# Message products of a graph network on two 64-column halves of TensorE, in place of 128 columns at once

## The chip, the core and the metric

The kernel runs on one NeuronCore of a Trainium2 chip. The core's engines work side by side, each through its own list of instructions: TensorE (PE) multiplies matrices on an array of 128 x 128 cells, with results in PSUM; VectorE (DVE) and ScalarE (ACT) work element by element; GpSimd (POOL) does a little of the same; SyncE (SP) starts DMA transfers. Semaphores order them. A matmul is two instructions, the load of its stationary operand (LDWEIGHTS, shown as PEld) and the multiplication that streams the moving operand through (MATMUL, shown as PE). The metric is the device time of the whole program in microseconds.

## What is computed

There are 16 graphs of 1024 nodes with 128 features, and each has its own 1024 x 1024 adjacency matrix. A first small network and a norm make `x` from the inputs. Then four layers follow, which have the same form and, in the third and fourth, wider inputs (features of earlier layers are put beside):

```python
IN_DIMS = [128, 128, 256, 384]
def _layer(nodes, adj, ws, bs, wd, bd, wn, bn, wu, bu):
    src = nodes @ ws + bs
    src_agg = jnp.einsum('bjv,bij->biv', src, _l2norm(adj, 2))
    dst = nodes @ wd + bd
    dst_agg = jnp.einsum('bjv,bji->biv', dst, _l2norm(adj, 1))
    self_rep = nodes @ wn + bn
    upd = jnp.concatenate([src_agg, self_rep, dst_agg], axis=2)
    return jnp.tanh(upd @ wu + bu)
...
x = _layernorm(x + _L1_gnn_ref(x, adj, ...), axis=-1)
```

All of it is in float32. The kernel folds `wu` into `ws`, `wd` and `wn` once, so that a layer is: **messages** (nodes times folded weights plus bias, 256 values for each node: 128 for the destination's sum and 128 for the source's), then the **aggregation** (messages times adjacency, both directions, plus the nodes' own part), then tanh.

## The kernel before

Per graph, TensorE goes through: messages of the first layer, aggregation, messages of the second, aggregation, messages of the third, aggregation, the first small network of the *next* graph, messages of the fourth, aggregation. Constants: `P = 128`, `V = 64`, `HW = 512`, `NJ = 4`, `CHUNKS = [1, 1, 2, 3]` (128-wide parts of a layer's input).

A helper issues one product as two, each for 64 of its 128 stationary columns. The output's partitions choose the half of the array:

```python
def by_halves(out, x, y, start=True, stop=True):
    for s in (slice(V, P), slice(V)):
        nc.tensor.matmul(out[s], x[:, s], y, start=start, stop=stop)      # L183
```

It serves several small sums (`pm`, `pv`, `pc`, `rp`, 32 columns to stream) and the weights of the small network (`pw`, 512 columns).

The messages. The stationary operand is 128 nodes of the features `f`, the moving one the 256 columns of the folded weights `wm`. Each group `g` makes two blocks of 128 nodes in one PSUM bank, which DVE reads when it adds the bias:

```python
def messages(b, l, feats, wm, between={}, with_sums=True):
    nch = CHUNKS[l]
    t = [one.tile([P, NJ, 2, 2, V], F32, tag=f"t{j}", ...) for j in range(2)]
    for n, g in enumerate((2, 3, 0, 1)):
        pt = ps_t.tile([P, 2, 2 * P], F32, tag="pt", ...)                 # ps_t: 4 banks
        for q in range(2):
            i = 2 * g + q
            for k, (f, c) in enumerate(feats):
                nc.tensor.matmul(pt[:, q], f[:, i * P:(i + 1) * P], wm[:, 1 + c],
                                 start=(k == 0), stop=(k == nch - 1))     # L605
        j, o = divmod(2 * g, NJ)
        nc.vector.tensor_add(t[j][:, o:o + 2]..., pt, wm[:, 0]...)        # L608
        if n in between:
            between[n]()
    ...
    for part in (DST, SRC):                                               # S3, L620
        nc.vector.tensor_sub(S[3][:, :, part], X[0, 0][:, :, part], X[1, 0][:, :, part])
    nc.vector.tensor_add(S[1], X[1, 0], X[1, 1])
    nc.vector.tensor_sub(S[2], S[1], X[0, 0])
    nc.vector.tensor_sub(S[4], X[0, 1], S[2])
    return X, S
```

The groups 2 and 3 need the second half of the nodes' features, 0 and 1 the first half.

The aggregation (Strassen's scheme in Winograd's form, with 64 message columns as one block) issues its products in pairs, one for each 64-column half of the array, with 512 columns to stream:

```python
def aggregate(b, l, feats, msgs, a, at, T, Q, fT, etag, hooks={}, pieces=1):
    ...
    upper = [(Z1, True, own(1, 1)), (Z0, True, own(1, 0)), (A, True, prod("M1", DST) + ...), ...]
    lower = [(Z1, True, own(0, 1)), (Z0, True, own(0, 0)), ...]
    up, lo = flat_steps(upper, high), flat_steps(lower, low)      # high: partitions 64..127
    for i, pair in enumerate(zip(up, lo)):
        if i - 2 * n in events:
            events[i - 2 * n]()            # DVE and ACT read finished products
        if i in hooks:
            hooks[i]()                     # work for other stages and the next graph
        for o, x, y, start, stop in pair:
            nc.tensor.matmul(o, x, y, start=start, stop=stop)             # L774
    nc.vector.tensor_add(e0, e0, Z0)                                      # L776
    squash(l, 0, e0, fT)                   # tanh of the first half on ACT, L787
```

It begins with the nodes' own part (`own`, one to three pairs for each half of the nodes), which needs no messages. The second half of the features is squashed before the aggregation ends, the first half after it.

The first graph's first layer alone is done by `plain_layer`, with products of 128 stationary columns (L653). The engines' instructions stay in the order in which the program issues them (`manual_schedule`).

Of the kernel before, what the change touches and what calls it, by code (L numbers as in the profile page):

```python
# [14 lines left out]
P = 128  # L15
# [8 lines left out]
def adj_resnorm_kernel(ctx: ExitStack, tc: tile.TileContext, x, adj, w0, b0, layers, out):  # L24
# [33 lines left out]
    nc = tc.nc  # L58
# [62 lines left out]
    def message_tile(name):  # L121

        return one.tile([P, 4, 2 * P], F32, tag="wm", name=name)
# [48 lines left out]
    def message_weights(b, l):  # L172
        wm = message_tile(f"wm{l + 1}_{b}")
        nc.sync.dma_start(wm[:, :CHUNKS[l] + 1], wsave[l])
        return wm

    def small(name, shape=(K,)):
        return ps_s.tile([P, *shape], F32, tag="small", name=name)
# [5 lines that stand above are left out]
# [411 lines left out]
    def messages(b, l, feats, wm, between={}, with_sums=True):  # L595


        nch = CHUNKS[l]
        t = [one.tile([P, NJ, 2, 2, V], F32, tag=f"t{j}", name=f"t{l + 1}_{b}_{j}") for j in range(2)]
        for n, g in enumerate((2, 3, 0, 1)):  # L600
            pt = ps_t.tile([P, 2, 2 * P], F32, tag="pt", name=f"pt{l + 1}_{b}_{g}")
            for q in range(2):
                i = 2 * g + q
                for k, (f, c) in enumerate(feats):
                    nc.tensor.matmul(pt[:, q], f[:, i * P:(i + 1) * P], wm[:, 1 + c],  # L605
                                     start=(k == 0), stop=(k == nch - 1))
            j, o = divmod(2 * g, NJ)
            nc.vector.tensor_add(t[j][:, o:o + 2].rearrange("p k a v c -> p k (a v c)"), pt,  # L608
                                 wm[:, 0][:, None, :].to_broadcast([P, 2, 2 * P]))
            if n in between:  # L610
                between[n]()
        if not with_sums:
            return t


        S = {i: one.tile([P, NJ, 2, V], F32, tag=f"S{i}", name=f"S{i}_{l + 1}_{b}") for i in (2, 3, 4)}
        X = {(v, j): t[j][:, :, :, v] for v in range(2) for j in range(2)}
        S[1] = X[1, 0]
        for part in (DST, SRC):
# [5 lines that stand above are left out]
# [203 lines left out]
    wm = message_tile("wm1_0")  # L828
# [27 lines left out]
    pt = small("w0tr", [HW])  # L856
# [139 lines left out]
    for b in range(B):  # L996
# [8 lines left out]
        if b == 0:  # L1005
            def row_factors0():
# [3 lines left out]
                for q in (2, 3):  # L1010
                    scale_rows(rows[q], q, rinv)

            t = messages(b, 0, feats, wm, {0: lambda: to_x1(0), 2: row_factors0}, with_sums=False)
            cinv = {}

# [42 lines left out]
            wm = message_weights(b, 1)  # L1058
            a2 = load(n)
            xs2 = load_spread(n)  # L1060
        else:
            w = {}
            if nxt:
                w["a"] = load(n)
                st = begin_sums(n)
            t = messages(b, 0, feats, wm)
            wm = message_weights(b, 1)
            Q = combined(b, "Q")
# [22 lines left out]
        feats = [(f1, 0)]  # L1091
        f23 = feature(b, "f23T")
        t = messages(b, 1, feats, wm)
        wm = message_weights(b, 2)

# [106 lines left out]
        wm = message_weights(b, 3)  # L1202
# [92 lines left out]
        if nxt:  # L1295
            wm = message_weights(n, 0)
# [60 lines left out]
```

## Time and profile before

| | |
|---|---|
| median of 3 runs | 2456.7 us (2456.55 to 2457.03) |
| span of the profiled run | 2454.6 us |
| TensorE's mean granted clock | 1.000 |
| TensorE busy | 2433.6 us (99%), 11453 matmul rows |
| LDWEIGHTS | 1026.5 us (42%), 11453 rows |
| DVE busy | 1909.8 us (78%) |
| ACT busy | 956.8 us (39%) |
| DMA | 41.3% of 16 engines for the data queue, 90 GB/s on average |
| messages (L605) | 1792 matmul rows of 128x256, mean 379 to 386 ns; loads of 128 columns, 190 ns |
| aggregation (L774) | rows of 128x512 on 64 columns, mean 592 to 602 ns; loads of 64 columns, 137 ns |

In a line of a group, `128*64` is the stationary operand's rows and columns, `128x512` the shape of what streams, then the number of rows, the busy time and the mean duration of one, the idle time of the engine just before them and who ended it. A float32 product of the program stands in the trace as two rows. Durations of matmuls overlap, since the next one starts before the last has left the array; the distance of two starts tells what one costs in a sequence. A load can run under the streaming of the matmul before it.

### The profile page before, as it was taken

To read this page: it belongs to the slowest core of one execution; us is meant where nothing else is said; L and a number is where in the kernel's file an instruction comes from. 1 tells how busy PE (TensorE), PEld (TensorE's weight loads), DVE (VectorE), ACT (ScalarE), POOL (GpSimd) and SP (SyncE) were. 2 spreads that over 40 slices of the span, in tenths; PEclk is the share of its full clock that TensorE was granted. 3 is DMA by queue.
4 is the path that set the end of the run, shared out by engine and by line. 5 is a ranking of instruction groups with operands and counts; after the bars stand their busy time and mean duration, and the time that the engine had idled before them with its cause. 6 is when DMAs were issued, how large, how long until landed. Compare 5 with 4: busy or idle time off the path is not lost.

```text
span 2454.6 us, 30806 instructions
## 1 busy us (share of the span) xinstructions
PE 2433.6 (99%) x11453; PEld 1026.5 (42%) x11453; DVE 1909.8 (78%) x2495; ACT 956.8 (39%) x1794; POOL 287.2 (12%) x100
## 2 busy tenths in 40 slices
PE   8999999999999999999999999999999999999998
PEld 5443344433444344443434434334443344433444
DVE  5878878798786878868788687887878878697743
ACT  5415334263342624335144351533515334262321
POOL 4101111101111011111011110111100111101100
PEclk9999999999999999999999999999999999999999
DMA  9517254261633517235172352724427254261410
GB/s 207 105 46 150 52 116 89 63 132 44 138 75 74 113 44 160 62 82 104 44 155 59 83 104 59 144 54 102 90 64 140 49 123 90 61 126 44 95 24 9
DMA packets 365717, 219.69 MB, mean 90 GB/s; under 512 B 152768, under 2 KB 336832, under 8 KB 365568
## 3 DMA queue, kind: packets, MB, share of 16 engines
q1 hardware_dynamic: 364800, 215.36, 41.3%
q0 software_dynamic: 768, 2.36, 0.4%
q8 instruction: 91, 1.49, 0.3%
q14 instruction: 58, 0.48, 0.1%
HBM read 199.17 MB, written 18.46 MB: 89 GB/s over the span
## 4 chain that ended last, share of the span: by engine, by line
PE 84%; DVE 6%; DMA 5%; SPq 1%; ACT 1%; issue 1%; DVEq 0%; POOLq 0%; ACTq 0%
PE m L774 37%; PE z L774 21%; PE pt L605 15%; PE m_f L516 5%; DMA a<-in_adj_dram 3%; PE pw L183 2%; PE z_f L516 2%; SPq L549 1%; DVE at L564 1%; DMA rows<-in_adj_dram 1%; DVE acc L262 1%; DMA rows_acc<-in_adj_dram 1%; DMA raw<-in_L_gnn_ws_dram 1%; DVE at L583 1%; DVE Q L587 0%
## 5 line engine op out<-in xcount | busy, mean ns | idle before, releaser
L774 PE MATMUL m<-Q,S 128*64 128x512 f32 x1008 | 445.0, 593 | 1.4 <-DVE Q L587 1.3
L387 POOL TENSOR_TENSOR rs<-ve,mhalf 128x32 f32<-128x32 f32 x30 | 205.2, 6840 | 1972.2 <-DVE ve L385 1972.2
L774 PE MATMUL m<-T,S 128*64 128x512 f32 x1008 | 394.9, 593 | 0.0
L774 PE MATMUL m<-at,t 128*64 128x512 f32 x1008 | 394.4, 593 | 0.0
L774 PE MATMUL m<-a,t 128*64 128x512 f32 x1008 | 391.7, 593 | 0.0
L608 DVE TENSOR_TENSOR t<-pt,wm 128x512 f32<-128x512 f32 x256 | 176.5, 690 | 171.4 <-PE pt L605 169.6
L774 PEld LDWEIGHTS m<-Q,S 128*64 128x64 f32 x1008 | 136.3, 137 | 281.9 <-issue 270.1
L687 ACT COPY e<-m 64x512 f32<-64x512 f32 x63 | 36.6, 582 | 510.7 <-PE m L774 510.4
L774 PE MATMUL z<-Q,t 128*64 128x512 f32 x504 | 229.3, 593 | 1.9 <-DVE Q L591 1.9
L774 PE MATMUL z<-a,t 128*64 128x512 f32 x504 | 229.5, 593 | 0.0
L774 PE MATMUL z<-a,S 128*64 128x512 f32 x504 | 227.0, 593 | 0.0
L774 PE MATMUL z<-at,S 128*64 128x512 f32 x504 | 226.7, 592 | 0.0
L774 PE MATMUL z<-at,t 128*64 128x512 f32 x504 | 226.6, 592 | 0.0
L605 PE MATMUL pt<-wm,f1T 128*128 128x256 f32 x768 | 213.7, 383 | 0.1
L774 PEld LDWEIGHTS m<-T,S 128*64 128x64 f32 x1008 | 120.1, 137 | 135.4 <-issue 135.4
L774 PEld LDWEIGHTS m<-at,t 128*64 128x64 f32 x1008 | 118.6, 137 | 135.9 <-issue 134.8
L774 PEld LDWEIGHTS m<-a,t 128*64 128x64 f32 x1008 | 119.1, 137 | 134.7 <-issue 121.5
L774 PE MATMUL z<-T,t 128*64 128x512 f32 x384 | 172.8, 592 | 0.0
L605 PEld LDWEIGHTS pt<-wm,f1T 128*128 128x128 f32 x768 | 143.2, 190 | 44.3 <-issue 13.5
L345 DVE TENSOR_TENSOR a<-a,cinv 128x512 f32<-128x512 f32 x250 | 154.1, 691 | 7.7 <-DMA cinv<-dr 5.4
L605 PE MATMUL pt<-wm,f23T 128*128 128x256 f32 x512 | 152.4, 379 | 1.1 <-ACT f23T L787 1.1
L253 ACT ACTIVATE sq<-a 128x1024 f32<-128x1024 f32 x120 | 125.7, 1048 | 69.4 <-DVE acc L262 63.2
(238 smaller groups left out, 4269.7 us busy)
## 6 DMA issues: line engine op xcount, KB each, us to landing
a<-in_adj_dram SPq DMA_DIRECT2D x120, 512.0 KB, 10.8
a<-in_adj_dram SPq DMA_DIRECT2D x240, 128.0 KB, 4.2
rows<-in_adj_dram SPq DMA_DIRECT2D x240, 64.0 KB, 2.7
wm<-wsave SPq DMA_DIRECT2D x16, 512.0 KB, 4.9
xn<-in_x_dram SPq DMA_DIRECT2D x124, 64.0 KB, 1.9
wm<-wsave SPq DMA_DIRECT2D x31, 256.0 KB, 3.5
xs<-in_x_dram SPq DMA_DIRECT2D x60, 128.0 KB, 3.6
cinv<-dr SPq DMA_DIRECT2D x30, 256.0 KB, 5.2
```

The lines of the kernel that those rows point to most:

```text
L183: nc.tensor.matmul(out[s], x[:, s], y, start=start, stop=stop)
L253: nc.scalar.activation(sq, a[:, i, :], AF.Square, accum_out=state["cols"][:, i:i + 1])
L262: nc.vector.tensor_add(state["acc"], state["acc"], state[i])
L345: engine.tensor_mul(a[:, i, s], a[:, i, s], cinv[:, s])
L387: nc.gpsimd.tensor_tensor(rstd, ve, mhalf[:, :n], ALU.pow)
L516: nc.tensor.matmul(o, x_, y_, start=start, stop=stop)
L549: queue.dma_start(piece[g * C:(g + 1) * C, :, h * P:(h + 1) * P], v[h, g, :, i * n:(i + 1) * n])
L564: nc.vector.transpose(at[h][:, j:j + NJ, c].rearrange("p j (k c) -> p j k c", c=C), piece.rearrange("p k (j c) -> p j k c", c=C)[:, j:j + NJ])
L605: nc.tensor.matmul(pt[:, q], f[:, i * P:(i + 1) * P], wm[:, 1 + c], start=(k == 0), stop=(k == nch - 1))
L608: nc.vector.tensor_add(t[j][:, o:o + 2].rearrange("p k a v c -> p k (a v c)"), pt, wm[:, 0][:, None, :].to_broadcast([P, 2, 2 * P]))
L687: nc.scalar.copy(e0[high], A[high])
L774: nc.tensor.matmul(o, x, y, start=start, stop=stop)
```

## The change

The product of the messages goes through the helper: each block of 128 nodes becomes a pair of 64 nodes each on the two column halves of the array, as the products of the aggregation on both sides of it are. What is computed, the order of the groups, the PSUM tiles and the work of the other engines stay. The purpose is that TensorE has one way of using its array throughout.

```diff
             for q in range(2):
                 i = 2 * g + q
                 for k, (f, c) in enumerate(feats):
-                    nc.tensor.matmul(pt[:, q], f[:, i * P:(i + 1) * P], wm[:, 1 + c],
-                                     start=(k == 0), stop=(k == nch - 1))
+                    by_halves(pt[:, q], f[:, i * P:(i + 1) * P], wm[:, 1 + c], k == 0, k == nch - 1)
             j, o = divmod(2 * g, NJ)
             nc.vector.tensor_add(t[j][:, o:o + 2].rearrange("p k a v c -> p k (a v c)"), pt,
                                  wm[:, 0][:, None, :].to_broadcast([P, 2, 2 * P]))
```

## Prediction, made before the changed kernel ran

> **What bounds the kernel now.** I read the page's first part (engine shares), then its second (clock), then the groups, and then the instructions of TensorE in order of time around one messages stage in the middle of the run, because the first three only say where to look.
>
> ```profile
> PE 2433.6 (99%) x11453; PEld 1026.5 (42%) x11453; DVE 1909.8 (78%) x2495; ACT 956.8 (39%) x1794; POOL 287.2 (12%) x100
> ...
> PEclk9999999999999999999999999999999999999999
> ...
> L774 PE MATMUL m<-Q,S 128*64 128x512 f32 x1008 | 445.0, 593 | 1.4 <-DVE Q L587 1.3
> ...
> L605 PE MATMUL pt<-wm,f1T 128*128 128x256 f32 x768 | 213.7, 383 | 0.1
> ```
>
> TensorE is busy 99% of the span at its full clock, and the matmul groups show next to no idle time. DVE (78%) and ACT (39%) only matter where TensorE waits for them. In the groups, `128*64` is a matmul on half of the array's columns and `128*128` one on all of them. Line 774 is the aggregation, which already runs as pairs of halves. Line 605 is the products that the change touches: 768 + 512 + 512 = 1792 rows. Each float32 product of the program stands as two rows, so that is 896 products: 16 graphs x 8 blocks x (1+1+2+3) chunks.
>
> A busy TensorE need not be streaming: a row's duration contains the pipeline's tail. So I take the spacing of starts. The timeline of TensorE where an aggregation hands over to the messages (start us, duration, engine, line, what):
>
> ```profile
> 1015.88 0.62 PE L774 MATMUL z<-Q,t 128*64 128x512 f32 x1
> 1015.92 0.62 PE L774 MATMUL z<-a,t 128*64 128x512 f32 x1
> 1016.34 0.59 PE L774 MATMUL z<-Q,t 128*64 128x512 f32 x1
> 1016.38 0.59 PE L774 MATMUL z<-a,t 128*64 128x512 f32 x1
> 1016.90 0.70 PE L605 MATMUL pt<-wm,f1T 128*128 128x256 f32 x2
> 1017.43 0.59 PE L605 MATMUL pt<-wm,f23T 128*128 128x256 f32 x2
> ```
>
> and where they hand back, 7 us later:
>
> ```profile
> 1023.04 0.59 PE L605 MATMUL pt<-wm,f1T 128*128 128x256 f32 x2
> 1023.48 0.59 PE L605 MATMUL pt<-wm,f23T 128*128 128x256 f32 x2
> 1024.00 1.08 PE L774 MATMUL z<-f1T,wown 128*64 128x512 f32 x4
> 1024.91 1.03 PE L774 MATMUL z<-f23T,wown 128*64 128x512 f32 x4
> ```
>
> Inside the stages the spacing is steady. Two half rows of 512 columns start side by side, and the next two follow 429 ns later. Full rows of 256 columns follow each other at 215.8 ns, so a product (two rows) takes 0.43 us. Each border is wider. Into the messages: the row at 1016.38 has streamed by 1016.81, the next starts at 1016.90, and the product after it comes 0.53 us later, not 0.43. Out of them: 1023.48 + 0.43 is 1023.91, but the next starts at 1024.00, and the pair after it comes at 0.91 instead of 0.86.
>
> **What the Trainium skill says.** "TensorE: Matmul & The Clock Gate", section "Back-to-back issue gap", gives N/2.4 + 2.5 ns per matmul. With two passes per row this is 2 x 256/2.4 + 2.5 = 215.8 ns and 2 x 512/2.4 + 2.5 = 429.2 ns; the trace agrees with both. So a full product and a concurrent pair of halves over the same 256 columns should take equal time. "TensorEngine Tiling (Array Packing)", section "Key Properties", says that changing the tiling mode, not just the tile, drains TensorE, and that tiles load and multiply independently. The trace agrees: about 95 ns stand free at every border between 128*64 and 128*128. Where a 128*64 pair of another shape comes in between, nothing stands free: a pair starting at 1005.48 is followed by `pv` at 1005.91, exactly 0.43 later.
>
> ```profile
> 1005.48 0.59 PE L774 MATMUL m<-Q,S 128*64 128x512 f32 x1
> 1005.48 0.59 PE L774 MATMUL z<-at,S 128*64 128x512 f32 x1
> 1005.91 0.26 PE L183 MATMUL pv<-v,fold 128*64 128x32 f32 x4
> ```
>
> The first page's section "LDWEIGHTS (loading the stationary operand)" gives columns/1.2: 107 ns for 128, 53 for 64. The trace is near it. After a border the second full row starts 320 ns after the first instead of 216, which is one exposed load of 104 ns. A half's two loads in a row start 60 ns apart (below).
>
> **The change, part by part.**
>
> Removed: 896 full products, 1792 rows of 215.8 ns = 386.7 us. Added: 896 pairs over the same 256 columns. If the halves run side by side as in the aggregation, 1792 row slots at 215.8 ns: difference 0. Loads double in number to 3584 but have half the columns.
>
> Removed too: the borders. I measured every messages stage from the end of the streaming before it to the start of the streaming after it. From the second graph on, all stages of a kind agree within a few ns: 3.800 us for 16 rows (first and second layer), 7.254 for 32 rows, 10.706 for 48. Less the rows at 215.8 ns (3.453, 6.906, 10.358), 0.347, 0.348 and 0.348 us remain: the same whatever the length, so a cost of the border. It is made of 0.095 drain + 0.105 exposed load going in, and 0.096 drain + 0.052 exposed load going out. With everything in halves there is no change of mode, and the next loads can be made under the streaming, as in the aggregation: all of it goes.
>
> There are 64 stages. In the first graph's first layer, which remains on the full array (`plain_layer`, line 653), the borders are not saved but moved to other places, some 0.5 us more. 62 stages save 0.347: 21.5 us. All of it lies on the path that sets the end, as TensorE works without a pause around them.
>
> **What takes back part of it** is data that was ready just in time. Going in, the second layer's third group of messages needs features that ACT finishes 0.27 us before TensorE gets there now. TensorE will come 0.2 us earlier, leaving 0.07 us, about one load of 0.06: at most 0.05 us x 16 = 0.8 us, in the third layer nothing (2 us to spare). Going out, the first aggregation product that needs DVE's sums starts 0.51 us after they are done in the first two layers, and 2 us in the last two; 0.15 us earlier still leaves 0.36. The DVE chain ahead of `pc` (it makes TensorE wait 0.27 us now) starts from a matmul inside the same aggregation and moves with it.
>
> Sum: 2456.7 - 21.5 + 0.5 + 0.4 = **2436 us**, 0.8% less.
>
> **The rivals.**
>
> *Loads become the bound.* A pair needs four loads in 431 ns, twice as many as now. Taken at the 137 ns that the load groups show each, and one after another, they need 548 ns: +117 ns x 896 = +105 us, 2562 less the borders: 2540. Against it stand the loads behind a short pair:
>
> ```profile
> 1032.69 0.14 PEld L774 LDWEIGHTS m<-at,t 128*64 128x64 f32 x1
> 1032.70 0.14 PEld L774 LDWEIGHTS m<-a,t 128*64 128x64 f32 x1
> 1032.75 0.14 PEld L774 LDWEIGHTS m<-at,t 128*64 128x64 f32 x1
> 1032.76 0.14 PEld L774 LDWEIGHTS m<-a,t 128*64 128x64 f32 x1
> ```
>
> 137 ns is latency. The two halves load 10 ns apart and each takes its next load 60 ns later, so four loads need some 120 ns of 431. Unlikely.
>
> *Issue becomes the bound.* Eight instructions in 431 ns is one per 54 ns, twice the present density, for up to 10.3 us. The first of the pages ("Step-by-step: what each phase is for", decoding) names 62 ns per matmul if the sequencer's program decodes them. If that held for loads too, a pair would take 496 ns: +58 us, 2494. Against it: the weights' folding (`wm`, line 166) starts a row every 110 ns, a load and a matmul, so one instruction per 55 ns, over six rows. And after the wait of `pc` at 1015.74, seven loads and the matmuls between start within 0.21 us. Neither shows it over 10 us, so some chance remains.
>
> *The halves don't overlap at 256 columns.* Then each product takes twice 431 ns: +386 us, about 2820. The pairs with 512 and with 32 columns do overlap, so I see no reason for it.
>
> *A wait takes the drain's place.* If ACT's features held the second layer's start fully (16 x 0.2 = 3.2 us) and DVE's sums the exits of the first two layers (31 x 0.15 = 4.6 us), the result would be 2443. The margins above speak against most of it.
>
> **Range and chances.** The main branch, about 0.9 of the weight, lies between 2435 (all borders gone) and 2443 (waits take a third). I allow 3 us below it for gains that I don't see, and take 2432 to 2443 for 8 in 10. More than 2% faster would need 49 us, more than twice all borders: 0.01. More than 2% slower needs the first three rivals: 0.05. Within 2%: 0.94.
>
> **What would show each step.** Right: the 1792 rows of line 605 become 3584 of the helper's line 183, `pt<-wm`, `128*64 128x256`; two start together, the next two 216 ns later; no free 0.09 us at the borders; a 16-row-slot stage takes 3.45 us; a graph takes 1.4 us less than its 150.4. Wrong: pair spacing above 216 ns with loads starting late (loads or issue), or first loads of groups held by ACT or DVE in the second layer. What I would have misjudged most is issue density: then the longest stage, the last layer's, would lose most.

## The result, and the profile after

| | before | after |
|---|---|---|
| median | 2456.9 us (4 runs, 2456.6 to 2458.2) | 2439.4 us (4 runs, 2436.4 to 2441.1) |
| ratio | | 0.9927, 95% interval 0.9909 to 0.9944 |
| span of the profiled run | 2454.6 us | 2438.5 us |

The change saves 17.5 us, 0.7%.

The page after, its first line and the groups of the messages:

```profile
PE 2415.8 (99%) x13245; PEld 1058.5 (43%) x13245; DVE 1909.6 (78%) x2495; ACT 957.1 (39%) x1794; POOL 287.1 (12%) x100
...
L183 PE MATMUL pt<-wm,f1T 128*64 128x256 f32 x1536 | 219.4, 380 | 0.0
...
L183 PE MATMUL pt<-wm,f23T 128*64 128x256 f32 x1024 | 160.5, 379 | 0.0
```

The products now stand under the helper's line 183, in twice as many rows. TensorE is still busy 99%: this line could not have told the gain beforehand, and doesn't show it now. The idle column doesn't either. The gain stands between the starts. The timeline of TensorE at the same two borders as before (graph 6, counted from 0, third layer), going in:

```profile
1011.78 0.59 PE L773 MATMUL z<-Q,t 128*64 128x512 f32 x1
1011.82 0.59 PE L773 MATMUL z<-a,t 128*64 128x512 f32 x1
1012.22 0.63 PE L183 MATMUL pt<-wm,f1T 128*64 128x256 f32 x4
1012.65 0.63 PE L183 MATMUL pt<-wm,f23T 128*64 128x256 f32 x4
```

and going out:

```profile
1018.69 0.63 PE L183 MATMUL pt<-wm,f23T 128*64 128x256 f32 x4
1019.12 1.06 PE L773 MATMUL z<-f1T,wown 128*64 128x512 f32 x4
1019.98 1.06 PE L773 MATMUL z<-f23T,wown 128*64 128x512 f32 x4
```

1011.78 + 0.43 is 1012.21, and the messages start at 1012.22. The next product follows 0.43 us later, not 0.53. Going out, 1018.69 + 0.43 = 1019.12, and the pair after it comes at 0.86. Nothing stands free any more. The loads are seen to have moved, too (TensorE's loads; the first two already start at 1011.79, under the aggregation's last rows):

```profile
1012.22 0.17 PEld L183 LDWEIGHTS pt<-wm,f1T 128*64 128x64 f32 x2 [0.26 <-issue]
1012.43 0.39 PEld L183 LDWEIGHTS pt<-wm,f23T 128*64 128x64 f32 x4
```

Where the time came from, by layer. Each number is the distance from the start of one layer's messages to the start of the next layer's, taken from the starts in the trace, for the graphs 1 to 14, which are alike:

| | before | after | saved over 14 graphs |
|---|---|---|---|
| first layer | 29.55 to 30.21 | 29.21 to 30.80 | 1.2 us |
| second layer | 30.25 to 30.26 | 29.92 (one 30.29) | 4.3 us |
| third layer | 50.29 | 49.94 | 4.9 us |
| fourth layer | 40.12 | 39.79 | 4.7 us |

With the last graph's 1.2 us, nothing from the first graph, and a start that came 0.3 us later, this makes the 16.1 us between the two spans. The second to fourth layer deliver 0.33 to 0.35 us per stage, with one exception: in graph 4 the second layer is 0.36 us longer than in the others. There DVE stood still for 0.47 us between two of its own additions, and the small product `pc` had to wait for its sum. Why is not shown. The first layer's shortest interval has shrunk by 0.34 us as well, but most of its intervals are longer than the shortest. Over the 14 graphs they exceed it by 2.7 us in the kernel before and by 6.2 in the one after, so that some 3.5 us of the 4.7 are lost.

Here is the worst of them, in graph 6 (30.80 us, 1.6 more than the shortest). SyncE's queue of transfers, then ACT, then DVE, then TensorE, of the kernel after:

```profile
952.53 0.31 SPq L196 DMA_DIRECT2D a<-in_adj_dram  x1
953.25 4.57 SPq L549 DMA_DIRECT2D rows_acc<-in_adj_dram  x8
957.88 4.55 SPq L196 DMA_DIRECT2D a<-in_adj_dram  x7
```

```profile
961.56 1.70 ACT L556 ACTIVATE rows_acc<-rows_acc,rinv 128x256 f32<-128x256 f32 x4 [5.30 <-DMA rows_acc<-in_adj_dram]
```

```profile
963.29 0.71 DVE L564 STREAM_TRANSPOSE at<-rows_acc 128x512 f32<-128x512 f32 x1 [1.46 <-ACT rows_acc L556]
```

```profile
964.06 0.64 PE L773 MATMUL m<-at,t 128*64 128x512 f32 x1 [0.34 <-DVE at L564]
971.95 0.64 PE L773 MATMUL m<-Q,S 128*64 128x512 f32 x1 [0.80 <-DVE Q L587]
```

(In brackets the idle time ahead and who ended it.) The aggregation needs the adjacency's rows too, transposed. The last eight row transfers of a graph, `rows_acc`, arrive when its first layer is already running; ACT scales them, DVE transposes them into `at` and makes the combinations `Q` from it, and TensorE waits for both. Told by the starts, it loses 0.58 us here at `at` and 1.01 us at `Q`, together the 1.6 us of this graph. ACT's 5.30 us is the longest wait, and most of it costs nothing; what gets through to DVE, 1.46 us, is what pushes `at` and `Q` back. The row transfers stand behind the first piece of the *next* adjacency, `a`, in the same queue. That piece cannot go before its buffer is free; the waits of SyncE's queue between 930 and 985 us (us in total, times, longest) have it:

```profile
SPq L196 <- DVE at L564: 7.2, 1, 7.2
```

So the rows wait for a buffer that they do not use.

### The profile page after: what moved, and what is told of

It is laid out like the page before. It is cut to its first block, busy times and chain, and to the rows that moved or that the text cites. A ratio compares the mean times of both kernels' runs of the same rounds, so it can differ in the third digit from the quotient of the medians.

```text
span 2438.5 us, 34361 instructions
## 1 busy us (share of the span) xinstructions
PE 2415.8 (99%) x13245; PEld 1058.5 (43%) x13245; DVE 1909.6 (78%) x2495; ACT 957.1 (39%) x1794; POOL 287.1 (12%) x100
## 4 chain that ended last, share of the span: by engine, by line
PE 78%; DMA 9%; DVE 8%; SPq 2%; issue 2%; ACT 1%; DVEq 0%; ACTq 0%; POOLq 0%
PE m L773 33%; PE z L773 20%; PE pt L183 14%; PE m_f L516 5%; DMA a<-in_adj_dram 5%; PE z_f L516 2%; PE pw L183 2%; DMA rows<-in_adj_dram 2%; DVE at L564 2%; SPq L549 2%; DMA rows_acc<-in_adj_dram 1%; DVE Q L587 1%; DVE at L583 1%; DVE T L591 1%; DMA raw<-in_L_gnn_ws_dram 1%
## 5 line engine op out<-in xcount | busy, mean ns | idle before, releaser
L183 PE MATMUL pt<-wm,f1T 128*64 128x256 f32 x1536 | 219.4, 380 | 0.0
L183 PE MATMUL pt<-wm,f23T 128*64 128x256 f32 x1024 | 160.5, 379 | 0.0
L183 PEld LDWEIGHTS pt<-wm,f1T 128*64 128x64 f32 x1536 | 121.7, 137 | 58.4 <-ACT f1T L786 12.0
```

## Experiments

Two theories were set against each other for the 4 us that are missing of the borders' 21.5 (the prediction had set aside 0.9 of them). A: the borders are worth what was predicted, and the first layer gives a part back by late rows. B: the doubled instructions cost it. A second set asks what the gain itself is made of.

**The change once more**, beside the next three.

> The change as it is, on the same chip as the next three. Theory A (the borders between array modes are gone, 0.34 us at each of 60 stages, and some 4 us of it are given back in the first layer, where adjacency rows arrive too late by DMA): 2439 us, between 2436 and 2441, with the first layer's interval anywhere from 29.2 to 31 us and the other layers' fixed. Theory B (the doubled number of TensorE instructions costs the 4 us, in the messages themselves or in instruction fetches): the same total, but the missing time spread over all layers.

2437.8 us (2437.1 to 2438.6), ratio 0.9923 (0.991 to 0.9935). The second to fourth layers are at 29.93, 49.94 and 39.79 us again, but for graph 4's second, which again takes 0.36 us more, and the first between 29.21 and 30.78. This time the worst is graph 8, not 6. So the first layer's loss isn't spread over the layers, as B has it, and it isn't tied to one graph. Only the 0.36 us of graph 4 stay in their place; they are outside of A, and there B isn't excluded.

**Rows first.** Only the order in SyncE's queue is changed, so that the rows no longer stand behind the waiting piece:

```diff
-                    queue.dma_start(piece[...], v[h, g, :, i * n:(i + 1) * n])
+                    newest[0] = queue.dma_start(piece[...], v[h, g, :, i * n:(i + 1) * n])
...
-                w["a"] = load(n)
+                with tc.issue_after(newest[0].ins):     # order of issue, no wait for landing
+                    w["a"] = load(n)
```

> The change, with the last eight row transfers of the next graph queued ahead of the first piece of the adjacency after it, which now stands before them in SyncE's queue and waits. Theory A: the first layer's interval is 29.2 us for every graph, 2434 us (2433 to 2435.5), and the runs lie closer together. Theory B: nothing in the instructions of TensorE changes, so 2439 us as the change itself.

2433.3 us (2432.6 to 2435.0), ratio 0.9906 (0.9891 to 0.9921). The first layer takes 29.21 to 29.23 us in every graph from 1 to 15. That the runs would lie closer together did not come true: from lowest to highest there are 2.4 us in four runs here, and 1.5 in five runs of the change beside it. SyncE's queue and ACT of this kernel:

```profile
945.94 3.92 SPq L551 DMA_DIRECT2D rows_acc<-in_adj_dram  x8
950.82 3.80 SPq L196 DMA_DIRECT2D a<-in_adj_dram  x8
```

```profile
954.45 1.69 ACT L558 ACTIVATE rows_acc<-rows_acc,rinv 128x256 f32<-128x256 f32 x4
```

The rows go out at 945.94, and all eight pieces of `a` follow when their buffer is free. No bracket is left at ACT's line: it goes on with the rows without a pause. A holds for the first layer, and B falls as the cause of its loss: the matmuls and loads of TensorE are the same (13245 of each in both profiles).

**Rows first in the kernel before.** The same edit on the full-width messages.

> The same new order of transfers in the kernel before, with full-width messages. Theory A: the first layer's waits there sum to 2.7 us (29.55 us is its shortest interval), so 2454 us, and the halves are worth 20 us under this order (2454 against 2434) where they were worth 17.5. Theory B: 2456.7, no difference.

2453.6 us (2453.2 to 2456.0), ratio 0.999 (0.9982 to 0.9998); the first layer takes 29.55 us in every graph. So the kernel before lost 2.6 us in the same way. With the rows out of the way on both sides, the halves are worth 2453.6 - 2433.3 = 20.4 us (the runs of each lie up to 2.8 us apart). The graphs 1 to 14 take 150.22 us there and 148.87 here (graph 4 takes 149.25): 1.35 less, or 0.34 for each of the four stages.

**The first layer left at full width.**

```diff
-                    by_halves(pt[:, q], f[:, i * P:(i + 1) * P], wm[:, 1 + c], k == 0, k == nch - 1)
+                    part = by_halves if l > 0 else by_whole
+                    part(pt[:, q], f[:, i * P:(i + 1) * P], wm[:, 1 + c], k == 0, k == nch - 1)
```

> The change in the second to fourth layer only; the first layer's messages keep 128 columns and their borders. Theory A: 45 stages save 0.34 us, the first layer keeps its interval of 29.55 us and the small waits of before: 2456.7 - 15.3 - 0.5 = 2441, nearly as good as the whole change, since the first layer's share of it is mostly given back. Theory B: three quarters of the 17.5 us, 2443.6.

2438.2 us (2437.7 to 2439.9), ratio 0.9925 (0.9913 to 0.9938): 18.0 us saved where A said 15.8 and B 13.1. A is nearer: the change in the first layer adds next to nothing to that in the other three. But A had the small waits of before stay, and they are gone in this profile: 29.45 us for every graph. The transfers are in the old order, and ACT still waits for the rows, 3.7 us per wait against 4.1 before, but DVE never waits for ACT. From DVE's first transposition of `rows_acc` to the first `Q` product there are 8.81 us here and 8.65 where TensorE is held, so a delay up to 0.16 us is free. In these graphs the delay was 0.11 at most. Why the rows came a little earlier in this kernel isn't settled.

**Four changes of mode in a stage.** From here on, all kernels have the rows first. They ran on another chip than the ones above, so each is compared with the runs of before beside it (2457.2 us there).

```diff
-                    by_halves(pt[:, q], ...)
+                    part = by_halves if n % 2 else by_whole      # n: group 0 to 3
+                    part(pt[:, q], ...)
```

> With the new order of transfers: of the four groups of each messages stage, the first and third at full width, the second and fourth in halves, so that half of the products are changed and a stage has four changes of mode where the kernel before has two. Theory A (the price is one of each change of mode): 0.35 us more per stage than full width throughout, 2453.6 + 62 x 0.35 = 2475 us. Rival (halves are cheaper per product, for their shorter loads): half of the gain of 20.4, 2443 us.

2476.4 us (2476.1 to 2476.7), ratio 1.0077 (1.0062 to 1.0092). Half of the products are changed, and the kernel is slower than with none changed: 19.2 us above its own runs of before, where full width with rows first was 2.6 below its own. A graph takes 151.62 us: 1.40 more than the 150.22 at full width, 0.35 per stage. It is the changes of mode that cost, not the width.

**Half of the products changed, two changes of mode.** The same edit with `n >= 2`.

> With the new order of transfers: the first two groups of each messages stage at full width, the last two in halves. Half of the products are changed, and a stage has two changes of mode as before, one at its start and one in its middle. Theory A: no gain, 2453.6 us (within 2). Rival (cheaper per product): 2443 us.

2454.6 us (2454.0 to 2456.1), ratio 0.9989 (0.9983 to 0.9996), 2.6 us below its own runs of before, just as full width with rows first; a graph takes 150.23 us. One border has moved from the stage's end to its middle, and nothing is gained.

**Quarters.**

```diff
-                    by_halves(pt[:, q], ...)
+                    by_quarters(pt[:, q], ...)       # four matmuls, 32 columns each
```

> With the new order of transfers: each product of the messages on four 32-column quarters of the array. Theory A (any change of tile mode drains): both borders are back, with about 0.095 us of drain each and an exposed load of 32 columns going in (0.03 to 0.05) and of 64 going out (0.05): 0.28 us x 62 = 17 us over halves throughout, 2451 us; inside the stages 216 ns for each row slot. Rival (only going between full and part width drains): 2433 us. If the issue of instructions has a limit above 27 ns each, the stages grow: at 54 ns a product takes 0.86 us, +385 us, 2820.

2451.0 us (2450.3 to 2451.8), ratio 0.9974 (0.9964 to 0.9984): 6.2 us below its runs of before, where halves were 23.0 below theirs, so 16.8 of the 20.4 us are lost again. TensorE's timeline going in:

```profile
1015.52 0.59 PE L780 MATMUL z<-Q,t 128*64 128x512 f32 x1
1015.55 0.59 PE L780 MATMUL z<-a,t 128*64 128x512 f32 x1
1016.08 0.64 PE L188 MATMUL pt<-wm,f1T 128*32 128x256 f32 x8
1016.53 0.61 PE L188 MATMUL pt<-wm,f23T 128*32 128x256 f32 x8
```

1015.55 + 0.43 is 1015.98, and the start at 1016.08 comes 0.10 later: the drain is back, though both sides use a part of the columns. So the change of tile size is what drains. A stage takes 3.74 us, 7.19 and 10.65 for the three lengths, 0.29 more than the rows' 3.453, 6.906 and 10.358. Full width had 0.347. The entrance is cheaper: the next product follows after 0.45 instead of 0.53, as a load of 32 columns is exposed there and not one of 128. So a border is a drain and an exposed load, as the prediction split it.

**Four times the instructions.** Halves, and each product in two of 128 moving columns:

```diff
-                for k, (f, c) in enumerate(feats):
-                    by_halves(pt[:, q], f[...], wm[:, 1 + c], k == 0, k == nch - 1)
+                for w in (slice(P), slice(P, 2 * P)):
+                    for k, (f, c) in enumerate(feats):
+                        by_halves(pt[:, q, w], f[...], wm[:, 1 + c, w], k == 0, k == nch - 1)
```

> With the new order of transfers: halves, and each product also split into two of 128 moving columns, so that there are four times the instructions of full width, in one mode throughout. Theory A (TensorE is held by streaming, 2.5 ns for each row, and nothing else): two more rows per half and product, 896 x 2 x 2.5 ns = 4.5 us over 2433.3: 2438 us, row slots 109 ns apart. Rival (loads or issue bind at this density; a half then loads every 109 ns, an instruction starts every 27 ns): at 54 ns an instruction 2820; if loads bind at 137 ns each, 2433 + 896 x 4 x 28 ns = 2534 us.

2438.5 us (2438.0 to 2438.7), ratio 0.9923 (0.9908 to 0.9937): 18.8 us below its runs of before, 4.2 less than halves in long rows. TensorE's timeline:

```profile
1011.66 0.42 PE L183 MATMUL pt<-wm,f1T 128*64 128x128 f32 x4
1011.87 0.42 PE L183 MATMUL pt<-wm,f23T 128*64 128x128 f32 x4
1012.09 0.42 PE L183 MATMUL pt<-wm,f1T 128*64 128x128 f32 x4
```

Four rows start every 0.218 us, with four loads beside them: one instruction per 27 ns, for up to 10.5 us. Compared with halves in rows of 256, the longest stage has become 0.12 us longer (10.457 against 10.337), which is 48 more row slots of 2.5 ns. Nothing but the rows' fixed cost has been added, and neither loads nor issue hold TensorE back at twice the density of the change. The 62 ns per matmul that the Trainium skill ("TensorE: Matmul & The Clock Gate", "Step-by-step: what each phase is for") gives for decoding by the sequencer's program, and that the prediction kept as a risk, do not bind here: a matmul starts every 54 ns, and a load beside it.

## Why the prediction was right

**Streaming.** "Difference 0" holds: pairs of 256 columns follow at 216 ns as full rows did, and the experiment with short rows fits a cost of 2.5 ns for each further row and no other.

**The borders.** 62 stages at 0.347 us, 21.5 us. Measured with the rows on time: 1.35 us for a graph's four stages where 1.39 was predicted, and 20.4 us in all. In the change itself, a graph takes 149.33 us on average, 1.08 less than before and not the 1.4 that the prediction named as a sign. With the rows first, and each against its own runs of before, no changes of mode in a stage stand at -23.0 us, two at -2.6 (both ways of having two), four at +19.2: two more cost 20.4 and 21.8 us. Drain and exposed load as parts of it are shown by the quarters.

**What takes it back** is the mis-sized term. The prediction had 0.9 us for it: 0.5 in the first graph and 0.4 for ACT's features in the second layer. The latter came as said: a second-layer stage takes 3.49 us, 0.04 more than its rows. The term as a whole measured 21.5 - 17.5 = 4 us, and in the profile 3.5 us of the loss lie in the first layer. The prediction looked at what TensorE waits for in messages (features, the messages' sums, `pc`) and found room in all of them. It did not follow the other operand of the aggregation, the transposed adjacency, back to its transfers. There the room was 0.16 us and is next to none after: from DVE's first transposition of `rows_acc` to the first `Q` product there are 8.81 us in the kernel before with rows first, and 8.64 in the one after, where 8.65 is the distance when TensorE is held. The room was, but for a little, the border at the stage's end (0.148 us). With two changes of mode, one of them in the middle of the stage and none at its end, the distance is 8.65 us too; with quarters, which have a border at the end, it is 8.78. So the time that the change takes out at the stage's end is the time that used to hide the late rows.

In the profile before, this stood open to see. The first layer's intervals, 29.55 to 30.21 us, were uneven, while those of the other layers agreed to 0.01, and ACT had a wait of 3.9 us for `rows_acc` in the graph whose border the prediction looked at. Behind it, DVE just didn't have to wait (ACT, then DVE, in the kernel before):

```profile
965.63 1.71 ACT L556 ACTIVATE rows_acc<-rows_acc,rinv 128x256 f32<-128x256 f32 x4 [3.90 <-DMA rows_acc<-in_adj_dram]
967.43 0.67 DVE L564 STREAM_TRANSPOSE at<-rows_acc 128x512 f32<-128x512 f32 x1
```

The prediction took "all stages of a kind agree" from the messages alone and did not ask it of the aggregations behind them.

**The rivals.** Loads, issue and halves that don't overlap are all refuted, by a run with twice the density of the change. "A wait takes the drain's place" is the rival that came about in part, about a fifth of the gain, but through an adjacency transfer in the first layer and not through features or sums. The range was wide enough for it, as it was drawn for waits of that size. That is in part luck, since the waits that it was drawn for did not come.

**A version that is better than both** came out of the experiments: the change with the rows first, 2433.3 us, 0.9% below the kernel before. Each edit brings more beside the other than alone: the order alone brings 2.6 us, the halves alone 17.5 (18.5 in the second measurement), both together 23.0.

## What to carry to other kernels

When TensorE is busy 99%, look at the distances of starts where the shape of its products changes. A border between tile sizes cost 0.15 to 0.2 us here whatever the length of the stage, so uniform tiles are worth most where stages are short and many. Before booking such a gain, follow both operands of the next products back to their transfers: a transfer that has room only because TensorE arrives late becomes the next wait. Here it stood in a queue behind another transfer's wait for a buffer, and moving it ahead was enough.

## What the runs showed of the hardware

A change between 64- and 32-column tiles drains TensorE just as one between 128 and 64 does (0.095 us each). Loads of float32 columns show 110, 137 and 190 ns for 32, 64 and 128 columns, which is 0.83 to 0.84 ns for each further column and some 83 ns that don't depend on them (an estimate from these three). Loads overlap enough that a load and a matmul every 54 ns were sustained for up to 10.5 us. The two halves of the array needn't run in step: in the change they stayed 35 ns apart through a whole stage (first rows at 1012.215 and 1012.250), after `pc` in the second layer had set them apart, and the stage took 6.906 us, just its rows at 215.8 ns.
